# Routed experts of a top-1 mixture: eight windows of 256 to 320 slots ordered by their counts, with the up weights standing still

## The chip, the cores and the metric

The kernel runs on one core of one Trainium2 chip. The metric is the device time of one execution in microseconds. The median of several runs is compared.

## The reference

Two blocks stand one behind the other, each added to a residual stream `x` of 16 x 128 tokens with 256 values each. The first is a cross attention of 16 heads. The second, which the change is about, is a mixture of eight experts with one expert per token, beside one expert that all tokens share (cut to what matters; `x_aD` holds the 2048 tokens after a layer norm):

```python
scores_aE = x_aD @ router_DE                       # 2048 x 8
vals_aK, idx_aK = jax.lax.top_k(scores_aE, 1)
masked_aE = jnp.full_like(scores_aE, -jnp.inf).at[jnp.arange(a)[:, None], idx_aK].set(vals_aK)
gates_Ea = jax.nn.sigmoid(masked_aE).T
routed_in_EaD = gates_Ea[:, :, None] * x_aD[None, :, :]
mid_EaF = silu(einsum('ead,edf->eaf', routed_in_EaD, w1_eDF)) * einsum('ead,edf->eaf', routed_in_EaD, w3_eDF)
routed_out_EaD = einsum('eaf,efd->ead', mid_EaF, w2_eFD)
shared_aD = silu(x_aD @ ws1_DF) * (x_aD @ ws3_DF) @ ws2_FD
out_aD = shared_aD + routed_out_EaD.sum(axis=0)
```

The inner width F is 704 = 5 x 128 + 64. All data are float32.

## The kernel before, in words

**Order.** The order of every engine's instructions is the order of the program text (`manual_schedule`). There is no planner. The attention part comes first, pair by pair of batch rows. The shared expert (`hidden`, L164, and `down`, L181) is cut into units that a generator hands out (`shared_expert`, L196; `shared_unit`, L249). Some units are put between the last steps of the attention, and the others between the steps of the routing.

**Weights.** `load_experts` (L913), right behind the attention, has SP load w1, w3 and w2 of all eight experts, one expert after the other, and they stay (`w13s`, `wds`).

**Routing.** `route` (L943) is a generator too. The loop at L1243 takes one step of it, or two where the first says "chain", and then one unit of the shared expert. Its steps are small DVE operations: the best score and its expert for each token (`hit`), the counts on TensorE (L1001), prefix sums over the 16 tiles of tokens (`run`), the number of 128-slot tiles of each expert (`tiles`, L1011), their prefix sum (`upto`) and first slot (`base`), each token's slot (`slot`), and from it the tile and the row in it (`tile_f`, `row`). `past` and `expert` (L1041 to L1050) name the expert of each tile. `there` and `sent` (L1054, L1063) and one-hot rows (`find`, L1073: `at_row`) go through TensorE (L1082) and become the table of token numbers and gates by slot.

**Routed tiles.** Each expert's tokens fill tiles of 128 slots; NTILE = 23 is the most that can be needed, and this input needs 20. The work of one tile is spread over the steps of `tiles` (L1272):

- `gather` (L1119, POOL) fetches the rows of the tokens from `h_rows`, `gate` (L1131, DVE) multiplies by the gates.
- The first two tiles are turned on TensorE (`transpose_inputs`, L1134). The others are turned by DVE in 32 x 32 blocks (`turn_inputs`, L1142), stored to a DRAM tensor `x_blocks` and read back in the other block order (`fetch_inputs`, L1153), both by SP.
- `up` (L1160): the turned tokens stand still (`lhsT=xT`), the weights move in halves of 352 columns: two halves x w1 and w3 x two chunks of 128 inputs. SiLU on ACT (L1179) and the product on DVE (L1180) leave the hidden rows by token.
- `turn_hidden` (L1183) and `fetch_hidden` (L1202) turn them in the same way: DVE, DRAM (`m_blocks`), and back.
- `out_rows` (L1208): POOL gathers the stream's rows from `s_rows`, TensorE multiplies the turned hidden rows with w2 (L1221, six blocks), DVE adds (L1228), and POOL scatters the rows to `out` (L1230). It runs two tiles behind `up`.

Sixteen tiles are sure. Behind them, a branch on the number of used tiles (L1311) runs either up to tile 20 or up to tile 23. Each branch ends with `ending` (L1290): the shared expert's last 256 tokens (`held`, L219) lie between the last two tiles' down products, and they are added to the rows that the scatters left in `out`: SP reads the rows back behind all scatters (L228), DVE adds (L246), SP stores (L247).

**PSUM.** Two double banks (`ps_s`: the halves of `up`), three banks (`ps_m`: the shared expert and the turns), one (`ps_o`: the down product).

Of the kernel before, what the change touches and what calls it, by code (L numbers as in the profile page):

```python
# [9 lines left out]
F32 = mybir.dt.float32  # L10
# [7 lines left out]
P = 128  # L18
# [3 lines left out]
G = 128  # L22
# [3 lines left out]
def resampler_attn__then__top1_moe_kernel(  # L26
# [31 lines left out]

    NSUB = NT // G + E - 1
    NTILE = -(-NSUB * G // P)  # L60
    GP = P // G
    TB = 2 * P
    FH = F // 2
# [3 lines left out]
    assert G == P and NF % 2 == 0 and FR == 2 * BL and F <= 512 * 2  # L67
# [842 lines left out]
    w13s = wexp.tile([P, E, DC, 2 * F], F32, name="w13s")  # L910
    wds = wexp.tile([P, E, NF, D], F32, name="wds")

    def load_experts():  # L913
        for e in range(E):
            for n, w in enumerate((w1, w3)):
                nc.sync.dma_start(
                    out=w13s[:, e, :, n * F : (n + 1) * F],
                    in_=w[e].rearrange("(c p) f -> p c f", p=P),
                )
            nc.sync.dma_start(  # L920
                out=wds[:, e, 0:FC, :],
                in_=w2[e, 0 : FC * P, :].rearrange("(c p) d -> p c d", p=P),
            )
            nc.sync.dma_start(
                out=wds[:, e, FC, :],
                in_=w2[e, F - P : F, :].rearrange("(j k) d -> k j d", k=BL),
            )

    routing = {}

    def prefix(a, n, width, name):

        k = 1
        while k < n:
            o = mscratch.tile([P, n * width], F32, tag=name, name=f"{name}{k}", bufs=2)
            nc.vector.tensor_copy(o[:, 0 : k * width], a[:, 0 : k * width])
            nc.vector.tensor_tensor(
                o[:, k * width :], a[:, k * width :], a[:, 0 : (n - k) * width], ALU.add
            )
            a, k = o, 2 * k  # L940
        return a

    def route():  # L943

# [6 lines left out]
        num_i = mscratch.tile([P, NTILE * GP], I32, tag="ints", name="num_i")  # L951
        nc.gpsimd.iota(num_i, pattern=[[1, NTILE * GP]], base=0, channel_multiplier=0)
        num = mscratch.tile([P, NTILE * GP], F32, name="num")
# [16 lines left out]
        col = mscratch.tile([P, P], F32, name="col")  # L970
# [4 lines left out]
        pay = mscratch.tile([P, B, 2], F32, name="pay")  # L975
# [5 lines left out]
        hit = mscratch.tile([P, B, E], F32, name="hit")  # L981
# [25 lines left out]
        run = prefix(cnt[:, 1, :], B, E, "run")  # L1007
        yield "chain"
        total = run[:, (B - 1) * E :]
        tiles_i = mscratch.tile([P, E], I32, name="tiles_i")  # L1010
        nc.vector.tensor_scalar(tiles_i, total, float(G - 1), None, ALU.add)  # L1011
        nc.vector.tensor_scalar(tiles_i, tiles_i, G.bit_length() - 1, None, ALU.arith_shift_right)
        tiles = mscratch.tile([P, E], F32, name="tiles")
        nc.vector.tensor_copy(tiles, tiles_i)
        yield "chain"
        upto = prefix(tiles, E, 1, "upto")
        base = mscratch.tile([P, E], F32, name="base")
        nc.vector.tensor_tensor(base, upto, tiles, ALU.subtract)
        nc.vector.tensor_scalar(base, base, float(G), None, ALU.mult)
        yield "chain"  # L1020

        pos = mscratch.tile([P, B, E], F32, name="pos")
# [3 lines left out]
        nc.vector.tensor_tensor(pos, pos, base.unsqueeze(1).to_broadcast([P, B, E]), ALU.add)  # L1026
        nc.vector.tensor_tensor(pos, pos, hit, ALU.mult)
        yield "chain"
        slot = mscratch.tile([P, B], F32, name="slot")
        nc.vector.tensor_reduce(slot, pos, AX.X, ALU.add)  # L1030
        tile_i = mscratch.tile([P, B], I32, name="tile_i")
        nc.vector.tensor_copy(tile_i, slot)
        nc.vector.tensor_scalar(tile_i, tile_i, 7, None, ALU.arith_shift_right)
        tile_f = mscratch.tile([P, B], F32, name="tile_f")
        nc.vector.tensor_copy(tile_f, tile_i)
        row = mscratch.tile([P, B], F32, name="row")
        nc.vector.scalar_tensor_tensor(row, tile_f, -float(P), slot, ALU.mult, ALU.add)
        yield "chain"

        past = mscratch.tile([P, NTILE * GP, E], F32, tag="grid", name="past")  # L1040
        nc.vector.tensor_tensor(  # L1041
            past,
            upto.unsqueeze(1).to_broadcast([P, NTILE * GP, E]),
            num.unsqueeze(2).to_broadcast([P, NTILE * GP, E]),
            ALU.is_le,
        )
        expert = mscratch.tile([P, NTILE * GP], F32, name="expert")
        nc.vector.tensor_reduce(expert, past, AX.X, ALU.add)
        expert_i = mconst.tile([P, NTILE * GP], I32, name="expert_i")
        nc.vector.tensor_scalar(expert_i, expert, float(E - 1), None, ALU.min)  # L1050
        yield "chain"

        there = mscratch.tile([P, B, NTILE], F32, tag="grid", name="there")
        nc.vector.tensor_tensor(  # L1054
            there,
            num[:, 0:NTILE].unsqueeze(1).to_broadcast([P, B, NTILE]),
            tile_f.unsqueeze(2).to_broadcast([P, B, NTILE]),
            ALU.is_equal,
        )
        yield  # L1060
        sent = mscratch.tile([P, B, 2, NTILE], F32, name="sent")
        for k in range(2):
            nc.vector.tensor_tensor(  # L1063
                sent[:, :, k, :],
                there,
                pay[:, :, k : k + 1].to_broadcast([P, B, NTILE]),
                ALU.mult,
            )
            yield
        pt = ps_o.tile([P, 2, NTILE], F32, tag="O", name="slots")  # L1070
        at_row = {}

        def find(b):  # L1073
            at_row[b] = rwork.tile([P, P], F32, tag="xg" if b % 2 else "xp", name=f"at_row_{b}")
            nc.vector.tensor_scalar(at_row[b], col, row[:, b : b + 1], None, ALU.is_equal)

        find(0)
        find(1)
        yield
        for b in range(0, B, 2):  # L1080
            for k in (b, b + 1):
                nc.tensor.matmul(  # L1082
                    pt.rearrange("p k j -> p (k j)"),
                    lhsT=at_row.pop(k),
                    rhs=sent[:, k].rearrange("p k j -> p (k j)"),
                    start=(k == 0),
                    stop=(k == B - 1),
                )
            if b + 2 < B:
                find(b + 2)  # L1090
                find(b + 3)
                yield
        table = mconst.tile([P, NTILE], I32, name="table")
        nc.vector.tensor_scalar(table, pt[:, 0, :], float(NT), None, ALU.add)
        gates = mconst.tile([P, NTILE], F32, name="gates")
        nc.vector.tensor_copy(gates, pt[:, 1, :])
        used_i = mconst.tile([P, 1], I32, name="used_i")
        nc.vector.tensor_copy(used_i, upto[:, E - 1 : E])
        routing.update(expert=expert_i, table=table, gates=gates, used=used_i)
        for j in range(AHEAD):  # L1100
            gather(j)
        for _ in range(4):
            yield
        for j in range(AHEAD):
            gate(j)
        yield
        for j in range(2):
            transpose_inputs(j)
        gather(AHEAD)
        turn_inputs(2)  # L1110


    AHEAD = 3

    SURE, SHORT = NT // P, 20
    xTs, ups = {}, {}
    x_blocks = [tc.dram_tile([DC, NB, BL, NB, BL], F32, name=f"x_blocks_{k}") for k in range(3)]

    def gather(j):  # L1119
        xg = rwork.tile([P, D], F32, tag="xg", name=f"xg_{j}")  # L1120
        nc.gpsimd.indirect_dma_start(
            out=xg,
            out_offset=None,
            in_=h_rows,
            in_offset=Offset(ap=routing["table"][:, j : j + 1], axis=0),
            bounds_check=NT,
            oob_is_err=False,
        )
        xTs[j] = xg

    def gate(j):  # L1131
        nc.vector.tensor_scalar(xTs[j], xTs[j], routing["gates"][:, j : j + 1], None, ALU.mult)

    def transpose_inputs(j):  # L1134
        xg = xTs[j]
        px = ps_m.tile([P, DC, P], F32, tag="mm", name=f"px_{j}")
        for c in range(DC):
            nc.tensor.transpose(px[:, c, :], xg[:, ts(c, P)], ident)
        xTs[j] = rwork.tile([P, DC, P], F32, tag="xp", name=f"xT_{j}")
        nc.vector.tensor_copy(xTs[j], px)  # L1140

    def turn_inputs(j):  # L1142

        px = rwork.tile([P, DC, NB, BL], F32, tag="xp", name=f"xp_{j}")
        nc.vector.transpose(
            px, xTs[j].rearrange("p (c k j) -> p c j k", c=DC, k=BL)
        )
        nc.sync.dma_start(
# [209 lines left out]
```

## Time and profile before

| what | value |
|---|---|
| median of 3 runs | 755.81 us (755.73 to 755.83) |
| the profiled execution | 755.33 us, of which its span 753.6 us |
| granted clock of TensorE | 0.999 |
| first routed up product | 582.9 us from the start of the span |
| TensorE's last group | from 744.04, 5.34 us long |
| DMA | 142.48 MB, mean 189 GB/s |

A row of a timeline has the start in us, the length in us, the engine, the line, the operation, what it writes and reads, and how many instructions were merged; in brackets the idle time of its engine ahead of it and what ended it. TensorE's work shows as PE (the product) and PEld (the load of the standing operand). Every float32 product leaves two records. In a row of groups the busy time and the mean of one record follow the first bar, the idle time ahead of the group and its releaser the second. A DMA row ends with the size of one transfer and the median time from issue to landing.

### The profile page before, as it was taken

How to read it: one execution, taken by the hardware profiler on the slowest of the kernel's cores; microseconds unless marked ns; L12 is line 12 of the kernel's file. 1: busy time of each engine (PE TensorE's matmuls, PEld its weight loads, DVE VectorE, ACT ScalarE, POOL GpSimd, SP SyncE). 2: the span in 40 equal slices, each digit the busy share in tenths (PEclk: the TensorE clock that was granted, in tenths of full speed). 3: DMA queues.
4: the chain of work that ended last, by engine and by line, in shares of the span. 5: the costliest groups of instructions: out<-in, count | busy, mean ns of one | idle time of the engine just before them, and what ended most of it. 6: DMA issues, size and time to landing. Idle time of an engine off the chain costs nothing.

```text
span 753.6 us, 11767 instructions
## 1 busy us (share of the span) xinstructions
PE 744.9 (99%) x4062; PEld 572.3 (76%) x4062; DVE 414.9 (55%) x1012; ACT 258.9 (34%) x779; POOL 315.2 (42%) x366
## 2 busy tenths in 40 slices
PE   8999999999999999999999999999999999999997
PEld 6857768778677677677677687788888777777776
DVE  5566558458558647656646456535633454554431
ACT  2444433534444354364354355611211111111111
POOL 1363653563464355345445544611022334343331
PEclk9999999999999999999999999999999999999999
DMA  8075636835844943953853544543996577777751
GB/s 294 32 251 184 195 127 211 238 139 174 258 143 157 263 168 131 259 199 125 235 196 128 182 155 174 175 140 118 383 381 242 147 209 190 185 184 192 189 154 55
DMA packets 182066, 142.48 MB, mean 189 GB/s; under 512 B 95152, under 2 KB 165811, under 8 KB 182004
## 3 DMA queue, kind: packets, MB, share of 16 engines
q1 hardware_dynamic: 175460, 125.07, 53.2%
q0 software_dynamic: 4528, 13.18, 5.6%
q10 hardware_dynamic: 2016, 3.43, 1.3%
q8 instruction: 35, 0.57, 0.3%
q14 instruction: 27, 0.22, 0.1%
HBM read 84.50 MB, written 57.67 MB: 189 GB/s over the span
## 4 chain that ended last, share of the span: by engine, by line
PE 78%; DMA 12%; issue 4%; DVE 3%; ACT 2%; POOL 1%; POOLq 0%; SPq 0%; DVEq 0%; ACTq 0%
PE pk L440 15%; PE pv L459 14%; PE S L492 8%; PE O L557 8%; PE p L156 8%; PE pw L573 7%; PE pq L425 7%; DMA out_dram<-sg,table 6%; DMA sg<-s_rows,table 5%; PE ys L186 5%; PE u L1169 3%; PE yr L1221 1%; ACT pe L511 1%; PE pr L628 1%; PE pr L156 1%
## 5 line engine op out<-in xcount | busy, mean ns | idle before, releaser
L524 POOL TENSOR_SCALAR pe<-pe,rs 128x256 f32<-128x256 f32 x256 | 233.0, 929 | 246.0 <-DVE rs L521 246.0
L511 ACT ACTIVATE pe<-S,nmx 128x256 f32<-128x256 f32 x256 | 118.9, 490 | 132.5 <-DVE nmx L504 132.5
L459 PE MATMUL pv<-wv,kvT 128*128 128x512 f32 x256 | 116.5, 599 | 0.2 <-ACT kT L448 0.2
L440 PE MATMUL pk<-kvT,wk 128*128 128x256 f32 x512 | 115.0, 382 | 1.3 <-ACT kT L448 0.7
L440 PEld LDWEIGHTS pk<-kvT,wk 128*128 128x128 f32 x512 | 95.9, 190 | 19.1 <-DVE px L533 2.0
L533 DVE STREAM_TRANSPOSE px<-pe 128x512 f32<-128x512 f32 x128 | 81.4, 683 | 32.5 <-POOL pe L524 32.4
L1169 PE MATMUL u<-w13s,xT 128*128 x320 | 97.8, 459 | 0.0
L459 PEld LDWEIGHTS pv<-wv,kvT 128*128 128x128 f32 x256 | 47.2, 190 | 53.2 <-issue 50.6
L1169 PEld LDWEIGHTS u<-w13s,xT 128*128 128x128 f32 x320 | 60.8, 190 | 30.7
L504 DVE TENSOR_REDUCE nmx<-S 128x4 f32<-128x1024 f32 x64 | 75.1, 1214 | 8.7 <-PE S L492 8.5
L156 PE MATMUL p<-hT,ws 128*128 128x256 f32 x320 | 73.8, 382 | 0.7 <-DVE mid L172 0.7
L156 PEld LDWEIGHTS p<-hT,ws 128*128 128x128 f32 x320 | 59.9, 190 | 10.6 <-DVE mid L172 1.7
L557 PEld LDWEIGHTS O<-pT,v 128*64 128x64 f32 x1024 | 55.2, 137 | 14.7 <-issue 12.9
L492 PE MATMUL S<-kT,qT 64*128 64x256 f32 x512 | 63.9, 389 | 0.0
L1179 ACT ACTIVATE rsl<-u 128x352 f32<-128x352 f32 x40 | 18.6, 464 | 130.6 <-PE u L1169 130.6
L557 PE MATMUL O<-pT,v 128*64 128x128 f32 x1024 | 63.0, 276 | 0.0
L521 DVE RECIPROCAL rs<-sums 128x4 f32<-128x4 f32 x64 | 11.4, 178 | 93.7 <-ACT pe L511 93.7
L466 ACT COPY v<-pv 128x512 f32<-128x512 f32 x64 | 38.2, 599 | 62.9 <-PE pv L459 62.9
L573 PEld LDWEIGHTS pw<-wo,oT 128*128 128x128 f32 x256 | 48.6, 190 | 12.2 <-issue 3.1
L573 PE MATMUL pw<-wo,oT 128*128 128x256 f32 x256 | 57.9, 379 | 0.0
L425 PE MATMUL pq<-kvT,wq 128*128 128x256 f32 x256 | 57.7, 379 | 0.0
L511 ACT ACTIVATION_READ_ACCUMULATOR pe<-S,nmx 128x1 f32 x256 | 56.5, 221 | 0.0
(203 smaller groups left out, 784.4 us busy)
## 6 DMA issues: line engine op xcount, KB each, us to landing
p_blocks<-px SPq DMA_DIRECT2D x64, 512.0 KB, 2.9
pT<-p_blocks SPq DMA_DIRECT2D x64, 512.0 KB, 4.2
w13s<-in_w_dram SPq DMA_DIRECT2D x16, 704.0 KB, 10.8
m_blocks<-body SPq DMA_DIRECT2D x20, 384.0 KB, 2.5
mT<-m_blocks SPq DMA_DIRECT2D x20, 384.0 KB, 4.0
wds<-in_w_dram SPq DMA_DIRECT2D x8, 640.0 KB, 12.4
t_blocks<-tx SPq DMA_DIRECT2D x12, 256.0 KB, 2.8
kvT<-t_blocks SPq DMA_DIRECT2D x12, 256.0 KB, 5.9
```

What stands on the lines that cost most here:

```text
L156: nc.tensor.matmul(ps, lhsT=shared["w13"][:, c, ds(col, P)], rhs=hT[:, c, ts(t, TB)], start=(c == 0), stop=(c == DC - 1),)
L425: nc.tensor.matmul(pq[:, jj], lhsT=wq[:, c, ts(2 * j + jj, P)], rhs=kvTs[g][:, c, :, 1, :], start=(c == 0), stop=(c == DC - 1),)
L440: nc.tensor.matmul(pk[:, jj, :], lhsT=wk[:, c, ts(2 * j + jj, P)], rhs=kvTs[b // 2][:, c, b % 2].rearrange("p t s -> p (t s)"), start=(c = ...
L459: nc.tensor.matmul(pv, lhsT=kvTs[b // 2][:, c, b % 2, t, :], rhs=wv[:, c, ts(n, 512)], start=(c == 0), stop=(c == DC - 1),)
L492: nc.tensor.matmul(pl[:, r, j, :], lhsT=qTs[b // 2][rows, k, b % 2, :], rhs=kTs[b][rows, k, :], start=True, stop=True,)
L504: nc.vector.tensor_reduce(nmx, pl, AX.X, ALU.max, negate=True)
L511: nc.scalar.activation(pes[u][:, h, :], pl[:, r, j, :], AF.Exp, bias=nmx[:, r, j : j + 1], accum_out=sums[u][:, h : h + 1],)
L524: nc.gpsimd.tensor_scalar(w, w, rs[:, i : i + 1], None, ALU.mult)
L533: nc.vector.transpose(px[:, :, t].rearrange("p j h q -> p h j q"), pes[u][:, ts(n, 4), ts(t, S)].rearrange("p h (j k) -> p h j k", k=BL),)
L557: nc.tensor.matmul(o[r * HD : (r + 1) * HD, j, :], lhsT=vs[b][:, t, ts(2 * (4 * half + j) + r, HD)], rhs=pTs[u][:, j // 2, :, t, 2 * (j % ...
L573: nc.tensor.matmul(pw, lhsT=outT[2 * b + k // 4][:, k % 4, :], rhs=wo[:, k, :], start=(k == 0), stop=(k == NP - 1))
L1169: nc.tensor.matmul(pl[:, m, 0:FH], lhsT=xT[:, c, :], rhs=w13s[:, ds(e, 1), c, ds(m * F + n * FH, FH)].rearrange("p e f -> p (e f)"), start ...
```

## The change

Each expert gets one **window** of slots. The windows have fixed sizes, 320, 288, 288, 288, 256, 256, 256 and 256, and the experts are put to them in the order of their counts, the largest first. A window consists of two tiles of 128 slots and, in the first four, a rest of 64 or 32; the sixteen full tiles have numbers 0 to 15 and the rests 16 to 19. If an expert has more tokens than its window has slots, a branch at the end takes the tokens beyond (`overflow`, up to 14 more tiles of 128).

- **Up products.** The weights stand still, in blocks of 128 columns, and the turned tokens of a whole window move. The hidden rows come out turned, as the down product needs them, so `turn_hidden`, `fetch_hidden` and `m_blocks` go. Block 5 holds the last 64 columns of w1 and of w3 side by side, and for this w3's columns are stored in another order.
- **Weights.** w2 of all experts is loaded ahead as before. w1 and w3 are loaded by SP for one window at a time into three buffers, the first three during the routing as soon as the experts are ordered, the others two windows ahead. SP reads the expert's number from a register.
- **Order in a window.** Behind the first block come the turning of the next window's inputs, the gathers for the window after it, the down products of the window before, the fetch of the next inputs and the load of weights. The down products' PSUM comes from `ps_m`.
- **Routing.** `tiles`, `upto`, `base`, `past` are replaced by ranks of the counts (`key`, `more`, `window`), by a place in the expert and a window for each token (`place`, `win`), by the tokens beyond (`over`) and by the largest load (`most`), on which the branch depends.
- **Ending.** `held` follows the last window; its first block comes before that window's down products, all others behind them.

The diff, cut to its core:

```diff
-G = 128
+WINDOWS = (320, 288, 288, 288, 256, 256, 256, 256)
...
-    w13s = wexp.tile([P, E, DC, 2 * F], F32, name="w13s")
     wds = wexp.tile([P, E, NF, D], F32, name="wds")
+    w13s = [wexp.tile([P, DC, 2 * F], F32, name=f"w13_{k}") for k in range(3)]
...
+        total = run[:, (B - 1) * E :]
+        key = mscratch.tile([P, E], F32, name="key")
+        nc.vector.scalar_tensor_tensor(key, total, float(2 * E), rank, ALU.mult, ALU.add)
+        more = mscratch.tile([P, E, E], F32, tag="grid", name="more")
+        nc.vector.tensor_tensor(
+            more,
+            key.unsqueeze(1).to_broadcast([P, E, E]),
+            key.unsqueeze(2).to_broadcast([P, E, E]),
+            ALU.is_gt,
+        )
+        window = mscratch.tile([P, E], F32, name="window")
+        nc.vector.tensor_reduce(window, more, AX.X, ALU.add)
+        yield "chain"
...
+        nc.vector.tensor_tensor(pos, pos, hit, ALU.mult)
+        own = mscratch.tile([P, B, E], F32, tag="own", name="own")
+        nc.vector.tensor_tensor(own, hit, window.unsqueeze(1).to_broadcast([P, B, E]), ALU.mult)
+        place = mscratch.tile([P, B], F32, name="place")
+        nc.vector.tensor_reduce(place, pos, AX.X, ALU.add)
+        win = mscratch.tile([P, B], F32, name="win")
+        nc.vector.tensor_reduce(win, own, AX.X, ALU.add)
+        yield "chain"
+        slot = mscratch.tile([P, B], F32, name="slot")
+        nc.vector.scalar_tensor_tensor(slot, win, 2.0 * P, place, ALU.mult, ALU.add)
...
+        over = beyond(place, win, B, "over", mconst)
...
+        for n, _ in enumerate(finding):
+            if n == 0:
...
+                nc.vector.tensor_copy(expert_i, expert)
+                for w in range(3):
+                    load_up(w, w)
+            if n == 1:
+                load = beyond(total, window, E, "load", mconst)
+                most = mscratch.tile([P, 1], F32, name="most")
+                nc.vector.tensor_reduce(most, load, AX.X, ALU.max)
...
+            yield
...
+        for i, t in enumerate(tiles_of(0)):
+            transpose_inputs(t, inputs_t[0][:, :, ds(i * P, rows_of(t))], rows_of(t))
+        for t in tiles_of(1):
+            gather(t)
...
+    def turn_inputs(w):
+        for i, t in enumerate(tiles_of(w)):
+            n = rows_of(t)
+            gate(t)
+            px = rwork.tile([P, DC, NB, BL], F32, tag="xp", name=f"xp_{t}")
+            nc.vector.transpose(
+                px[0:n], xgs.pop(t)[0:n, :].rearrange("p (c k j) -> p c j k", c=DC, k=BL)
+            )
+            nc.sync.dma_start(
+                out=x_blocks[:, ds(i * NB, n // BL)].rearrange("c i k j q -> (i k) c (j q)"),
+                in_=px[0:n].rearrange("p c j q -> p c (j q)"),
+            )
+
+    def fetch_inputs(w):
+        n = WINDOWS[w]
+        for c in range(DC):
+            nc.sync.dma_start(
+                out=inputs_t[w % 2][:, c, 0:n].rearrange("p (i q) -> p i q", q=BL),
+                in_=x_blocks[c, 0 : n // BL].rearrange("i k j q -> (k j) i q"),
+            )
+
+    def load_up(k, w):
+        e = nc.sync.value_load(routing["expert"][0:1, w : w + 1], min_val=0, max_val=E - 1)
+        a1, a3 = (a[ds(e, 1)].rearrange("e (c p) f -> p (e c) f", p=P) for a in (w1, w3))
+        nc.sync.dma_start(out=w13s[k][:, :, 0:F], in_=a1)
+        nc.sync.dma_start(out=w13s[k][:, :, F : F + FR], in_=a3[:, :, FC * P : F])
+        nc.sync.dma_start(out=w13s[k][:, :, F + FR : 2 * F], in_=a3[:, :, 0 : FC * P])
+
+    def up(w13, xT, n, mid, f, name):
+        ps = ps_s.tile([P, 2, 512], F32, tag="S", name=f"u_{name}_{f}")
+        sl = mwork.tile([P, WMAX], F32, tag="sl", name=f"rsl_{name}_{f}")[:, 0:n]
+        for k, col in enumerate((f * P, F + FR + f * P) if f < FC else (FC * P,)):
+            for c in range(DC):
+                nc.tensor.matmul(
+                    ps[:, k, 0:n],
+                    lhsT=w13[:, c, ds(col, P)],
+                    rhs=xT[:, c, 0:n],
+                    start=(c == 0),
+                    stop=(c == DC - 1),
+                )
+        if f < FC:
+            nc.scalar.activation(sl, ps[:, 0, 0:n], AF.Silu)
+            nc.vector.tensor_tensor(mid[:, f, 0:n], ps[:, 1, 0:n], sl, ALU.mult)
+        else:
+            hi = slice(P - FR, P)
+            nc.scalar.activation(sl[hi, :], ps[0:FR, 0, 0:n], AF.Silu)
+            nc.vector.tensor_tensor(mid[hi, FC, 0:n], ps[hi, 0, 0:n], sl[hi, :], ALU.mult)
...
+    for w in range(E):
+        ups[w] = nc.tensor.value_load(
+            routing["expert"][0:1, w : w + 1], min_val=0, max_val=E - 1
+        )
+        for f in range(NF):
+            up(w13s[w % 3], inputs_t[w % 2], WINDOWS[w], mids[w % 2], f, f"w{w}")
+            if f == 0:
+                sgs = [stream_rows(t, rows_of(t)) for t in tiles_of(w - 1)] if w else []
+                if w + 1 < E:
+                    turn_inputs(w + 1)
+                if w + 2 < E:
+                    for t in tiles_of(w + 2):
+                        gather(t)
+                if w:
+                    down_window(w - 1, sgs)
+                else:
+                    shared_unit()
+                if w + 1 < E:
+                    fetch_inputs(w + 1)
+                if 1 <= w < E - 2:
+                    load_up((w + 2) % 3, w + 2)
+
+    def ending():
+        rest = held(mids[E % 2][:, :, 0:TB])
+        sgs = [stream_rows(t, rows_of(t)) for t in tiles_of(E - 1)]
+        next(rest)
+        down_window(E - 1, sgs)
+        for _ in rest:
+            pass
...
+    with tc.If(most <= 2 * P) as cmp:
+        ending()
+    with cmp.Else():
+        scattered[:] = done
+        overflow()
+        ending()
```

`stream_rows` is the gather from `s_rows` that `out_rows` did before; `down_window` calls `out_rows` for the two or three tiles of a window; `tiles_of` and `rows_of` give a window's tiles and their rows.

## The prediction, before the changed kernel was run

> **What bounds the kernel now.** I read the page first: its busy line, then its costliest groups. TensorE is busy for nearly the whole span, and the routed part is 320 records of the up product (L1169) and 240 of the down product (L1221).
>
> ```profile
> PE 744.9 (99%) x4062; PEld 572.3 (76%) x4062; DVE 414.9 (55%) x1012; ACT 258.9 (34%) x779; POOL 315.2 (42%) x366
> ...
> L1169 PE MATMUL u<-w13s,xT 128*128 x320 | 97.8, 459 | 0.0
> ...
> L1169 PEld LDWEIGHTS u<-w13s,xT 128*128 128x128 f32 x320 | 60.8, 190 | 30.7
> ...
> L156 PE MATMUL p<-hT,ws 128*128 128x256 f32 x320 | 73.8, 382 | 0.7 <-DVE mid L172 0.7
> ```
>
> The last number of each row is the idle time before that group. The up product waits for nothing. A mean of 459 ns per record is no price, since records overlap. The price is the pace, which the timeline of TensorE alone gives from one start to the next:
>
> ```profile
> 692.75 4.90 PE L1169 MATMUL u<-w13s,xT 128*128 x16
> 697.48 2.75 PE L1221 MATMUL yr<-wds,mT 128*128 x12
> 700.07 4.90 PE L1169 MATMUL u<-w13s,xT 128*128 x16
> ...
> 733.68 7.07 PE L156 MATMUL p<-hT,ws 128*128 128x256 f32 x32
> 740.59 2.75 PE L1221 MATMUL yr<-wds,mT 128*128 x12
> ```
>
> Sixteen up records take 697.48 - 692.75 = 4.73 us, 0.2956 each with 352 moving columns. Twelve down records take 2.59, 0.2158 each with 256. The shared expert's 32 take 6.91, also 0.2159 each with 256. So a record costs 0.2158 us plus 0.831 ns for each column over 256 (0.0798/96). The stage has no gap until the end: its length is the sum of TensorE's records, and anything that DVE, the queues or the DMAs save there is worth nothing.
>
> **The up product.** Each product shows as two records. Before: 20 tiles x 16 records x 0.2956 = 94.6 us. After: the weights stand, and a window's slots move. A window has 11 column blocks of 128 (1408 in all), 2 chunks, 2 records: 44. At 320, 288 and 256 columns the formula gives 0.2690, 0.2424 and 0.2158 us. The sum is 44 x (0.2690 + 3 x 0.2424 + 4 x 0.2158) = 44 x 1.8594 = 81.8 us. **Gain 12.8 us.** In columns: 352 x 2208 against 320 x 352, 14% fewer. The reason is the last block: 64 columns of w1 and 64 of w3 share one stationary block, and slots are padded less.
>
> Here a rule speaks against the change. Perfetto Trace Analysis, "Identifying the Most-Contended Engine", says that matmul occupancy is a bad measure of headroom and that the share of time spent loading weights is the good one. The change adds 32 loads and shortens the move that covers each: by that rule, at 190 ns a load, 6.1 us are added. The row decides: L156 has the planned form (128 weights standing, 256 moving) and keeps 0.2159 with its 190 ns loads. The move, not the load, sets the pace; I take the 12.8.
>
> **The down product.** Before 20 tiles, after 16 full tiles and 4 short ones (64, 32, 32, 32 rows). The 256 weight columns still move through each, so a short tile costs a whole 12 x 0.2158. 20 x 2.59 both times: 0. The four short tiles save nothing.
>
> **Work taken off.** The turn of the hidden rows (DVE, 80 transposes at L1189 and L1193, 34.7 us in the groups of this stage), its 20 stores and 20 fetches and 12 of TensorE's 20 register loads go. All lay beside TensorE: 0.
>
> **New waits in the up product.** The blocks rotate through two PSUM pairs, and the last block of a window is short (4 records), so the next window's first block asks for a pair that was filled only 4 records before. The shared expert shows how long an evacuation takes:
>
> ```profile
> 737.34 0.38 ACT L171 ACTIVATE sl<-p 128x256 f32<-128x256 f32 x1 [1.34 <-PE p L156]
> 737.75 0.42 DVE L172 TENSOR_TENSOR body<-p,sl 128x256 f32<-128x256 f32 x1 [1.00 <-ACT sl L171]
> ```
>
> That block's 8 records end at 733.68 + 16 x 0.2158 = 737.13; SiLU starts 0.21 later and DVE's product ends at 738.17, 1.04 after the end. Restarting TensorE took about 0.16 (DVE ended at 574.97, the next group started at 575.03 and ran 0.10 longer). Inside a window 1.20 fits into a block's 1.73. At the boundary only 4 x 0.2158 = 0.86 covers it: 0.33 us idle. With 288 and 320 slots SiLU and product grow (up to 0.46 and 0.52 at 352), the short block too: 0.28 and 0.24. Seven boundaries: 0.24 + 3 x 0.28 + 3 x 0.33 = **+2.1 us**. Bounds: 0 if the framework frees a pair earlier, 3.5 if restarting costs twice as much.
>
> TensorE's register load stands at the same boundary, behind the short block. It is dispatched once the block before has started its last 0.7 us, so 0.7 + 0.86 + 0.33 = 1.9 us cover it. No row shows one alone. The nearest is the old branch near 705 us, whose load and jump held POOL 1.6 us and DVE 0.9: 0, at worst +0.5 at a boundary if the cover is gone. The new branch ahead of the ending has 1.55: 0, at worst 0.5.
>
> **The route.** The loop has as many steps as before (23 of 25 units), but DVE's steps are heavier. Before, DVE was nearly the limit:
>
> ```profile
> 533.49 8.80 PE L156 MATMUL p<-hT,ws 128*128 128x256 f32 x40
> ...
> 534.30 0.16 DVE L1011 TENSOR_SCALAR tiles_i<-run 128x8 int32<-128x8 f32 x1
> ...
> 542.12 1.03 PE L156 MATMUL pr<-hT,ws 128*128 128x256 f32 x4
> ...
> 542.74 0.42 DVE L172 TENSOR_TENSOR mid<-p,sl 128x256 f32<-128x256 f32 x1 [0.64 <-ACT sl L171]
> 543.08 0.47 DVE L1075 TENSOR_SCALAR at_row<-col,row 128x128 f32<-128x128 f32 x2
> ...
> 543.41 0.64 PE L1082 MATMUL slots<-sent,at_row 128*128 128x46 f32 x4 [0.26 <-DVE at_row L1075]
> ```
>
> From 534.30 to the row search DVE is idle for 0.64 us only. By the pitch of starts, an operation on up to 16 values costs 0.20, on 64 values 0.24, on 128 values 0.32, on 320 to 368 some 0.5. The old tiles, prefix and base lasted 1.86; the new key, ranks, places and windows (3 small, 6 of 128) 2.58. Slot steps: 2.33 against 2.84 (14 small). Grid and expert: 1.30 against 1.40. Payload: 0.45 against 1.68, since six small steps for the experts' loads lie there. That is +2.5; less the idle 0.64, the row search starts 1.9 us later and TensorE's slots product, which waits for it in order, with it. **+1.9 us**; bounds 0.5 and 2.5.
>
> **First window.** Three transposes instead of two take all three ps_m buffers. TensorE already waited 0.49 us there for DVE's L172; now the third transpose takes that buffer and the next block waits for DVE's first copy, 0.36 later, plus 0.1 of transposes: **+0.5**, bounds 0 and 1.
>
> **Weights in order.** SP first loads w2 (6.3 MB, from 522.5 to some 539 at 381 GB/s), then waits for the experts' names (about 541.7 us), then loads three pairs of w1 and w3 (1.44 MB each). At the same 381 GB/s these land near 541.7 + 11.4 = 553, needed near 584: 0. Behind SP's wait stand only window 1's stores, 30 us later. A later pair has nearly two windows (over 28 us); at this stage's 190 GB/s it needs 8. 0.
>
> **Window inputs.** They still go through DRAM, now just in time. The page's DMA rows:
>
> ```profile
> x_blocks<-xp SPq DMA_DIRECT2D x18, 128.0 KB, 3.7
> xT<-x_blocks SPq DMA_DIRECT2D x18, 128.0 KB, 4.2
> ```
>
> For windows 6 and 7, counted from the end of the first block: product 1.04, two gates and turns 2.0, store 3.7, two fetches 4.2 and some 2 for the second = 12.9 us. Cover: two down tiles 5.2, the other blocks 36 x 0.2158 = 7.8, the gap 0.3 = 13.3. It just fits; longer windows leave more. 0, but with the slowest landings (5.0 and 5.0) windows 6 and 7 would be 2.2 late each, window 1 2 and windows 2 to 4 0.7: up to +8.5.
>
> **The end.** Before, the last scatter started at 744.09, and reading it back made DVE's last add wait:
>
> ```profile
> 749.09 0.42 DVE L246 TENSOR_TENSOR xr<-ys,xr 128x256 f32<-128x256 f32 x1 [4.01 <-DMA xr<-out_dram]
> 749.54 1.47 SPq L247 DMA_DIRECT2D out_dram<-xr  x2
> 749.75 0.42 DVE L246 TENSOR_TENSOR xr<-ys,xr 128x256 f32<-128x256 f32 x1 [0.24 <-DMA xr<-out_dram]
> ```
>
> TensorE's last group ends at 744.04 + 5.34 = 749.38. After, five blocks (7.8 us) stand behind the last down tile, so the rows are back before and the add starts at once: -0.33, and the second store no longer queues behind the first. **-0.5**, bounds -0.8 and 0.
>
> **Sum.** -12.8 + 2.1 + 1.9 + 0.5 - 0.5 = -8.8 us. The profiled execution took 755.33 (span 753.6 and 1.7 around it), so 746.5; it lay 0.5 below the median of the runs, 755.81, so **747.0 us**.
>
> **Rivals.** (1) No bubbles: a pair comes free early and the route's extra DVE work hides, leaving -12.8 to -12.3, 743.3 us. For it: seldom more than one engine is late here. Against it: DVE's single 0.64. 17%. (2) Some covers fail: a few window inputs or register loads are late, +3.5 us, 750.5. For it: 0.4 us of room at windows 6 and 7. 20%. (3) Slower: the trip of the window inputs through DRAM becomes the bound. A window's fetch is issued after its stores have landed, so each window can start late by itself. Beyond 8.8/7 = 1.3 us on each of seven starts the gain is gone; 2.2 on each gives 15.4 - 8.8, 762.4. Against it: only the slowest landings on record, all at once, reach break-even, and the queue now carries no hidden rows. 5%; a further 3% ends near no change. (4) That the overflow path runs: the reference's router on its inputs gives 312, 286, 264, 262, 239, 232, 228 and 225 tokens, which fit the windows in order. Fourteen tiles at 44 x 0.109 + 2.6 = 7.4 us would add over 100; I leave it out.
>
> **How the numbers follow.** The sum as worked out has 55%. The range from 742.8 to 751.0 holds it with rival 1 and most of rival 2, and leaves out the rest. About 0.2% (1.5 us) is what a measurement can tell from no change. Faster 0.92, same 0.03, slower 0.05.
>
> **What would show it.** Right: 352 up records at 0.216 to 0.269 us, 240 down records at 0.216, gaps of about 0.3 us ahead of each window's first block released by DVE's product, a gap of 2 us ahead of the slots product, no wait of DVE's last add for the DMA. Wrong: up records at another pace, a window's start released by the DMA of its inputs, or w13 waited for.

## The result, and the profile after

The changed kernel takes 748.42 us (748.27 to 748.73, 4 runs) against 755.82 beside it: a ratio of 0.9902, 95% interval 0.9885 to 0.9919. The forecast was 747.0, range 742.8 to 751.0. The profiled execution took 748.45 with a span of 746.6; the span fell by 7.0 us.

The page after, its busy line and the two rows of the up product:

```profile
PE 736.0 (99%) x4096; PEld 572.5 (77%) x4096; DVE 385.8 (52%) x949; ACT 259.1 (35%) x787; POOL 314.4 (42%) x366
...
L1249 PE MATMUL u_w<-xT,w 128*128 128x256 f32 (+2 forms) x352 | 85.6, 399 | 0.3
L1249 PEld LDWEIGHTS u_w<-xT,w 128*128 128x128 f32 x352 | 66.0, 190 | 18.8 <-DVE mid_w L1258 3.3
```

TensorE is as full as before. The 352 up records are there, and now their weight loads wait for DVE. The view of waits (what waited, for whom, us in total, times, longest) has

```profile
PEld u_w L1249 <- DVE mid_w L1258: 3.3, 7, 0.5
```

A load runs ahead of the products, so TensorE itself loses less than the 3.3 us: 2.12, as experiment 3 shows. DVE's busy time fell by 29 us, and none of that shows in the span.

The timeline of TensorE gives the lengths by starts. The first and the last row are the first up product and the last shared down product. Between them stand a window of 288 slots with its neighbours' down products, then windows of 256 up to the ending:

```profile
584.11 2.32 PE L1249 MATMUL u_w<-xT,w 128*128 128x320 f32 x8
...
622.39 8.05 PE L1279 MATMUL yr<-wds,mid_w 128*128 x36
630.37 11.23 PE L1249 MATMUL u_w<-xT,w 128*128 128x288 f32 x44
641.43 8.05 PE L1279 MATMUL yr<-wds,mid_w 128*128 x36
...
698.37 10.00 PE L1249 MATMUL u_w<-xT,w 128*128 128x256 f32 x44
708.21 5.34 PE L1279 MATMUL yr<-wds,mid_w 128*128 x24
713.39 7.93 PE L1249 MATMUL u_w<-xT,w 128*128 128x256 f32 x36
721.16 1.89 PE L162 MATMUL p<-hT,ws 128*128 128x256 f32 x8
...
735.83 5.34 PE L245 MATMUL ys<-wsd,mid_w 128*128 128x256 f32 x24
```

A row of 44 holds five blocks of one window and the first of the next, so the boundary lies in it. The last row of 36 holds none: 721.16 - 713.39 = 7.77 = 36 x 0.2158, the pace of the formula exactly. The rows with a boundary are longer than their records: 9.84 instead of 9.50, and 11.06 instead of 10.67. The 36 down records of a three-tile window take 630.37 - 622.39 = 7.98, where 36 x 0.2158 is 7.77.

The other places that the prediction named: the slots product in the timeline of TensorE, the window inputs in the view of DMA issues of the routed part (transfer size and median time to landing at the end), and the end in the timeline of all engines.

```profile
542.42 1.03 PE L162 MATMUL pr<-hT,ws 128*128 128x256 f32 x4
544.29 0.64 PE L983 MATMUL slots<-sent,at_row 128*128 128x40 f32 x4 [0.84 <-DVE at_row L976]
```

```profile
x_blocks<-xp SPq DMA_DIRECT2D x14, 128.0 KB, 2.0
...
xT<-x_blocks SPq DMA_DIRECT2D x8, 128.0 KB, 3.0
```

```profile
739.08 2.93 SPq L253 DMA_DIRECT2D out_dram<-xr  x2
741.22 0.42 DVE L252 TENSOR_TENSOR xr<-ys,xr 128x256 f32<-128x256 f32 x1 [2.17 <-PE ys L245]
```

TensorE waits for DVE's row search, 0.84 us instead of 0.26. The inputs land sooner than before, and no row of TensorE waits for them. The last add waits for TensorE and no longer for the DMA.

The span's change, put together from starts of TensorE's rows:

| stretch | before | after | change | forecast |
|---|---|---|---|---|
| start to the first up product | 582.90 | 584.11 | +1.2 | +2.4 |
| first up product to the last shared down product | 161.14 | 151.72 | -9.4 | -10.7 |
| from there to the end of the span | 9.56 | 10.77 | +1.2 | -0.5 |

Of the first +1.2, 0.3 was there by 16 us, in the loading of the first inputs; in the runs below it was 0.1 to 0.9, so it belongs to no edit. Ahead of the slots product 0.6 were lost, at the third transpose 0.3. The second stretch repeats well: it is 151.72 or 151.73 us in the changed kernel, in its repetition and in experiments 1 and 5, which leave it as it is. So a difference of a few hundredths can be read there, while the intervals of the ratios below hardly part edits that lie 1.5 us from each other.

### The profile page after: what moved, and what is told of

It reads as the page before. It is cut to its first block, busy times and chain, and to the rows that moved or that the text cites. A ratio compares the mean times of both kernels' runs of the same rounds, so it can differ in the third digit from the quotient of the medians.

```text
span 746.6 us, 11560 instructions
## 1 busy us (share of the span) xinstructions
PE 736.0 (99%) x4096; PEld 572.5 (77%) x4096; DVE 385.8 (52%) x949; ACT 259.1 (35%) x787; POOL 314.4 (42%) x366
## 4 chain that ended last, share of the span: by engine, by line
PE 93%; DVE 4%; ACT 2%; issue 0%; DMA 0%; ACTq 0%
PE pk L446 15%; PE pv L465 14%; PE u_w L1249 11%; PE S L498 8%; PE O L563 8%; PE p L162 8%; PE pw L579 7%; PE pq L431 7%; PE yr L1279 7%; PE ys L192 5%; ACT pe L517 1%; PE pr L634 1%; PE pr L162 1%; PE ys L245 1%; PE slots L983 0%
## 5 line engine op out<-in xcount | busy, mean ns | idle before, releaser
L1249 PE MATMUL u_w<-xT,w 128*128 128x256 f32 (+2 forms) x352 | 85.6, 399 | 0.3
L1249 PEld LDWEIGHTS u_w<-xT,w 128*128 128x128 f32 x352 | 66.0, 190 | 18.8 <-DVE mid_w L1258 3.3
L1257 ACT ACTIVATE rsl_w<-u_w 128x256 f32<-128x256 f32 (+2 forms) x40 | 16.0, 400 | 118.8 <-PE u_w L1249 118.8
```

The source lines that it names most:

```text
L1249: nc.tensor.matmul(ps[:, k, 0:n], lhsT=w13[:, c, ds(col, P)], rhs=xT[:, c, 0:n], start=(c == 0), stop=(c == DC - 1),)
```

## The experiments

Each is an edit of the changed kernel. The ratio is to the kernel before, with its 95% interval.

**1. Where does the end go?** DVE's last add no longer waits for the DMA, as forecast. Still the program ends later. The raw records of SP show what stands between (start in us, length, operation, line of the branch or of the program's end):

```
before   751.07   0.04 COMPARE_BRANCH   L1311
         751.57   0.02 EVENT_SEMAPHORE  L1354
after    742.41   0.04 COMPARE_BRANCH   L1432
         745.02   0.02 EVENT_SEMAPHORE  L1474
```

Behind its last store SP leaves the branch by a jump over the other side, and its next instruction comes 0.5 us later before, 2.6 us later after. The DMA view of the changed kernel from 741 us on has the queues that load instructions:

```profile
q1 hardware_dynamic: 144, 0.13, 7.9%
q14 instruction: 3, 0.02, 1.4%
q8 instruction: 1, 0.02, 1.0%
```

The first experiment leaves the branch away:

```diff
-    (_, (most,)) = nc.values_load_multi_w_load_instructions(
-        routing["most"][0:1, 0:1], min_val=1, max_val=NT
-    )
     done = list(scattered)
-    with tc.If(most <= 2 * P) as cmp:
-        ending()
-    with cmp.Else():
-        scattered[:] = done
-        overflow()
-        ending()
+    ending()
```

> The branch and the overflow path are left out (no token of this input lies beyond its window), so the ending follows the last window directly. Theory 'jump': in the changed kernel SP leaves the branch by a jump over the overflow code, 2.6 us pass before its next instruction, and the program's closing waits start that much later. Without it the stretch from DVE's last add to the end of the span falls from 5.0 us to about 3.0, the time from 748.4 to about 746.4. Rival 'store': the last store's landing sets the end. Then nothing changes: 748.4, the stretch stays at 5.0.

Measured: 746.73 us, 0.9878 (0.9861 to 0.9894). The same DMA view has one queue left:

```profile
q1 hardware_dynamic: 144, 0.13, 10.4%
```

From TensorE's last group to the end there are now 744.8 - 735.85 = 8.95 us instead of 10.77. "Jump" holds, "store" falls: the loss is 1.8 us. It is less than 2.6 because a part of the jump lay beside the last store: without the branch SP waits at this place from 742.14 to 743.41, and the last packets of the store end at 743.05. So the end alone would have changed by 8.95 - 9.56 = -0.6, where -0.5 was forecast.

**2. The sides of the branch exchanged.**

```diff
-    with tc.If(most <= 2 * P) as cmp:
-        ending()
-    with cmp.Else():
-        scattered[:] = done
-        overflow()
-        ending()
+    with tc.If(most > 2 * P) as cmp:
+        overflow()
+        ending()
+    with cmp.Else():
+        scattered[:] = done
+        ending()
```

> The two sides of the branch change places: the overflow side stands first, the usual side last, so that the usual path jumps on entry and runs out of the program's end without a jump. Theory 'jump': the end gains what the kernel without overflow gains, some 2 us; on entry TensorE has 1.55 us of queued work to cover a jump of up to 2.6, so up to 1.0 is lost there: 746.4 to 747.4. Rival 'store': 748.4, or slower by a gap of TensorE ahead of the ending.

Measured: 750.98 us (748.99 to 751.71), 0.9936 (0.9920 to 0.9953): a miss. The end is 747.2 - 738.25 = 8.95 us long, as expected, but the timeline of TensorE shows the entry:

```profile
713.18 7.93 PE L1249 MATMUL u_w<-xT,w 128*128 128x256 f32 x36
723.47 1.99 PE L162 MATMUL p<-hT,ws 128*128 128x256 f32 x8 [2.35 <-issue]
```

TensorE's own jump lasts 3.5 us by its record (719.88 to 723.42), not 2.6, and only the five records queued behind its start, 1.1 us, covered it. This wait with the label "issue" is such time: no semaphore is late. The kernel before had shown the size: by the raw records TensorE's jump at its end lasts 3.75 us (from 745.36), hidden by 17 queued records. The profiled execution is the fastest of the four, 748.99; why the others took some 2 us more no trace here shows.

**3. The pair of banks at the window's boundary.**

```diff
-        ps = ps_s.tile([P, 2, 512], F32, tag="S", name=f"u_{name}_{f}")
+        if f < FC:
+            ps = ps_s.tile([P, 2, 512], F32, tag="S", name=f"u_{name}_{f}")
+        else:
+            ps = ps_m.tile([P, 1, 512], F32, tag="mm", name=f"u_{name}_{f}")
```

> The short block 5 of each window takes one of the three ps_m banks and no longer one of the two pairs, so the next window's first block finds a pair whose product ended a whole block earlier. Theory 'pair': the seven gaps of 0.25 to 0.44 us ahead of each window's first block, 2.6 us in all, are waits for DVE's product on block 4: they go, 745.9 us. Rival 'register': they are TensorE's load of the expert's number at the same place: they stay, 748.4.

Measured: 746.33 us, 0.9871 (0.9854 to 0.9887). The seven waits for DVE are gone from the view of waits, and the timeline of TensorE has

```profile
697.05 9.66 PE L1252 MATMUL u_w<-xT,w 128*128 128x256 f32 x44
706.54 5.34 PE L1282 MATMUL yr<-wds,mid_w 128*128 x24
```

9.49 for 44 records, the pure pace. From the first up product to the last shared down product there are 734.17 - 584.57 = 149.60 us instead of 151.72: the seven gaps were 2.12 us. "Pair" holds; the register load, in the same place, costs nothing. With 288 slots 0.1 us a window stays, which the next experiment explains.

**4. The narrow standing blocks of the rests.**

```diff
-    mids = [hidden_t.tile([P, NF, WMAX], F32, name=f"mid_w{k}") for k in range(2)]
+    mids = [hidden_t.tile([P, NF, 3 * P], F32, name=f"mid_w{k}") for k in range(2)]
...
+        nc.gpsimd.memset(mid[:, :, 2 * P : 3 * P], 0.0)
...
-                py[0:n, :],
-                lhsT=mid[:, f, 0:n],
+                py,
+                lhsT=mid[:, f, 0:P],
...
-            out_rows(t, rows_of(t), ups[w], mids[w % 2][:, :, ds(i * P, rows_of(t))], sg)
+            out_rows(t, rows_of(t), ups[w], mids[w % 2][:, :, ts(i, P)], sg)
```

> The down products of the four rests of 64 and 32 slots run with a standing block of full width (128 columns, the ones beyond the rest cleared once and their results not read). Theory 'shape': a narrow standing block costs 0.21 to 0.23 us beside the 2.59 of a whole tile[...]; with full width the 36 records of a three-tile window take 7.77 us instead of 7.98 to 8.00, and the time falls by 0.85 to 747.6. Rival 'third tile': three tiles in a row cost it for another reason (a PSUM bank, an add): 748.4, 7.98 us stays.

Measured: 747.51 us, 0.9887 (0.9871 to 0.9904). The timeline of TensorE around the same window:

```profile
641.18 7.93 PE L1279 MATMUL yr<-wds,mid_w 128*128 x36
648.95 10.91 PE L1249 MATMUL u_w<-xT,w 128*128 128x288 f32 x44
```

The down products take 648.95 - 641.18 = 7.77. The up row behind them, too, is 0.11 shorter than in the changed kernel. The stretch of the table is 734.95 - 584.51 = 150.44 us, 1.28 shorter: 0.32 for each of the four rests, 0.21 in its own records and 0.11 in those behind. The view of waits of the changed kernel names four waits at each of the two places, and none of them is left here:

```profile
PEld u_w L1249 <- issue: 1.6, 4, 0.4
PEld yr L1279 <- issue: 1.3, 4, 0.3
```

"Shape" holds in place and is half as large again as expected. The time is only 0.9 lower: the profiled execution has a start 0.4 us longer than the changed kernel's, which the edit doesn't touch, and of the other runs there is no trace. That the width of the standing block costs this is shown by the edit; why it does is not, as the trace's label is "issue".

**5. Two pieces of the routing later.**

```diff
-            if n == 0:
+            if n == 4:
                 named = mscratch.tile([P, E, E], F32, tag="named", name="named")
...
-            if n == 1:
+            if n == 6:
                 load = beyond(total, window, E, "load", mconst)
```

> The naming of the experts (with the first three loads) comes four steps of the routing later and the largest load five, behind the first row searches. Theory 'DVE': TensorE's wait of 0.84 us ahead of the first slots product comes from these two pieces, some 2.1 us of DVE time in a stretch where DVE has no idle time; moved, the wait falls to the 0.26 of the kernel before or less, the time by some 0.6 to 747.8. Rival 'PE': the row search waits for the product on TensorE's own last block in any order; the wait stays at 0.8, 748.4. The first weights then land some 9 us later, near 562, still 20 us early.

Measured: 748.07 us, 0.9896 (0.9879 to 0.9912). In the timeline of TensorE the wait ahead of the slots product is back at the value of before:

```profile
543.06 1.03 PE L162 MATMUL pr<-hT,ws 128*128 128x256 f32 x4
544.35 0.64 PE L983 MATMUL slots<-sent,at_row 128*128 128x40 f32 x4 [0.26 <-DVE at_row L976]
```

"DVE" holds, with 0.6 us in the trace (the changed kernel's wait was 0.84). In the time itself 0.4 are too near the spread of the runs to prove it (the start of the profiled execution happened to be 0.6 us longer). The next experiment bears it out from another side: its windows are of one size, so four small DVE steps fall away, and the wait there is 0.27 us.

**6. All windows of 320 slots.**

```diff
-WINDOWS = (320, 288, 288, 288, 256, 256, 256, 256)
+WINDOWS = (320,) * 8
```

> All eight windows have 320 slots: same weights standing, same 352 records, more columns. Theory 'columns': a record costs 0.2158 us plus 0.831 ns a column over 256, so 352 records at 0.2690 are 94.7 us against 81.8, +12.9; four more rests at 12 x 0.2158 and 0.32 for the narrow block, +11.6; boundary gaps 0.4 shorter: 772.5. Rival 'records': the number of products and loads sets the up product; it stays, and only the rests add: 760.

Measured: 772.1 us, 1.0219 (1.0202 to 1.0236). "Columns" holds within 0.4 us. The 2560 slots are as many as the 20 tiles of before have, and by the formula the up product is then as long as before, 94.7 us against 94.6. So in the up product standing weights gain nothing by themselves; the gain is the slots that the smaller windows leave out (2208). The 16 us above the kernel before are, by an estimate from the figures above, for the larger part the four more tiles of the down product (10.4 us) and eight narrow blocks (2.6).

**7. Do the loads set the pace?**

```diff
     def up(w13, xT, n, mid, f, name):
         ps = ps_s.tile([P, 2, 512], F32, tag="S", name=f"u_{name}_{f}")
+        n = P
...
-        nc.gpsimd.memset(mid[0 : P - FR, FC, :], 0.0)
+        nc.gpsimd.memset(mid, 0.0)
```

> The up products move only the first 128 slots of each window; the hidden rows of all other slots are left at zero, so their part of the computation is left out. Every weight load stays, with 128 columns to cover it. Rule 'load' (loads of 190 ns set the pace): records 0.190 us apart inside a block, about 731 us. Theory 'move': 0.2158 - 128 x 0.00083 = 0.109 us apart inside a block; the blocks of 0.88 then wait for the 1.2 us of evacuation, about 1.04 each, and the time falls to some 715.

Measured: 726.5 us, one run. The timeline of TensorE at the last window:

```profile
694.97 4.31 PE L1250 MATMUL u_w<-xT,w 128*128 128x128 f32 x36
699.13 1.99 PE L162 MATMUL p<-hT,ws 128*128 128x256 f32 x8
```

36 records start within 4.16 us, 0.116 each; the first block of all (584.66 to 585.55) had 0.111. That is near the formula's 0.109, and far from 0.190. The loads are all there, and by the page's row one is longer than this pace, so they overlap each other:

```profile
L1250 PEld LDWEIGHTS u_w<-xT,w 128*128 128x128 f32 x352 | 45.5, 205 | 17.9 <-DVE mid_w L1259 7.9
```

So "load" falls, by the pace; the time alone would not tell, as 726.5 lies nearer to 731 than to 715. It is 11 us above what "move" expected, and the view of waits has


```profile
PE u_w L1250 <- DVE mid_w L1259: 6.2, 9, 2.2
PE u_w L1250 <- DVE sg L1287: 2.9, 1, 2.9
PE u_w L1250 <- DMA xT<-x_blocks: 2.3, 2, 1.4
PE u_w L1250 <- issue: 1.7, 1, 1.7
```

With less work to cover them, waits that the prediction costed at nothing come forward: 13.1 us, of which 9.1 are for DVE (its product on a block, and once behind its add for the down product), 2.3 for the windows' inputs and 1.7 have no releaser. "Move" itself had put in some 0.16 us of waiting for each block, so how much of the 11 us each of them makes is not settled.

**8. The branch ahead of the last window's later blocks.** The usual side stands last, as in 2.

```diff
                 if 1 <= w < E - 2:
                     load_up((w + 2) % 3, w + 2)
+            if w == E - 1:
+                break
+
+    def last_window():
+        w = E - 1
+        for f in range(1, NF):
+            up(w13s[w % 3], inputs_t[w % 2], WINDOWS[w], mids[w % 2], f, f"w{w}")
...
-    with tc.If(most <= 2 * P) as cmp:
-        ending()
-    with cmp.Else():
-        scattered[:] = done
-        overflow()
-        ending()
+    with tc.If(most > 2 * P) as cmp:
+        last_window()
+        overflow()
+        ending()
+    with cmp.Else():
+        scattered[:] = done
+        last_window()
+        ending()
```

> The branch stands behind the first block of the last window and the down products of the window before it, with the overflow side first and the usual side last. Theory 'jump': on entry 24 queued records of 5.2 us cover TensorE's jump of 3.5, and the program ends without one: the stretch from the last add to the end is 3.1 us instead of 5.0, TensorE has no gap of 2.4, 746.6 us. Rival 'other engines': a jump of DVE, SP or POOL of the same size delays the product on the next block and TensorE waits for it up to 2 us: 748.5.

Measured: 748.0 us, 0.9897 (0.9881 to 0.9914): neither theory in full. The end is 746.3 - 737.37 = 8.93 us, but in the timeline of TensorE two gaps have come:

```profile
714.16 3.69 PE L1249 MATMUL u_w<-xT,w 128*128 128x256 f32 x16 [0.45 <-PE yr L1279]
718.27 4.58 PE L1249 MATMUL u_w<-xT,w 128*128 128x256 f32 x20 [0.41 <-DVE mid_w L1258]
```

By the records TensorE's sequencer reaches the branch at 710.09, when 8 of the 24 queued records have run, and jumps until 713.92; the rest of the queue covers only 3.5 us of that. DVE jumps from 714.87 to 717.72 and is late with the next product. The gain is 1.8, the loss 1.4: the stretch of the table is 153.10 us instead of 151.72.

**9 to 11. Together.** Edits 3, 4 and 5; the same with 8; the changed kernel once more.

> Three edits together on the changed kernel: the short block in a ps_m bank, the rests' standing blocks at full width, the naming and load steps of the routing later. If the three losses (2.1 us of boundary gaps, 1.3 of narrow blocks, 0.6 ahead of the slots product) are separate, as each theory has it, they add: 4.0 less than the changed kernel, 744.4. Rival 'one cover': removing one lets another wait (window inputs, at windows 6 and 7) come forward; then 745.5 or more and a wait for the inputs' DMA.

> The three edits and the branch ahead of the last window's later blocks. Alone, the early branch gained 1.9 at the end and lost 1.4 to the jumps on entry (TensorE 3.8 us, DVE 2.9). If these add: 0.4 below the kernel with the three edits, 744.0. Rival: with the pair's wait gone the entry costs the same or more, no gain, 744.4 or above.

> The changed kernel itself, once more, beside the two: 748.4, and 0.990 of the kernel before.

Measured: 744.54 us, 0.9852 (0.9837 to 0.9867); 743.88 us, 0.9842 (0.9828 to 0.9855); 748.49 us, 0.9902 (0.9887 to 0.9917). The three losses add (3.95 us below the changed kernel beside it, 4.0 expected), and no new wait takes their place. The stretch of the table, with the three edits,

```profile
583.35 2.32 PE L1252 MATMUL u_w<-xT,w 128*128 128x320 f32 x8
...
731.67 5.34 PE L245 MATMUL ys<-wsd,mid_w 128*128 128x256 f32 x24
```

is 148.32 us, 3.40 shorter than in the changed kernel, where 2.12 and 1.28 were found alone. The early branch adds some 0.7. The intervals overlap, but all five of its runs (743.80 to 744.04) lie below the four without it (744.16 to 745.11). Its trace agrees: the stretch is 1.36 us longer, at 149.68, and the end 1.91 shorter, 8.92 instead of 10.83. The version with all four is the fastest of all and beats both kernels.

## Why the prediction was right, point by point

- **Up product, -12.8: right.** The sum is borne out by the stretch itself: -12.78 + 2.12 (experiment 3) + 1.28 (experiment 4) = -9.4, as measured; with both losses gone it is 148.32 - 161.14 = -12.82. Experiment 6 changes the columns and the number of rests and lands within 0.4 us; experiment 7 rules out that loads of 190 ns set the pace. Two points of its working do not hold. The columns are 44 x 2208, not 352 x 2208, against 320 x 352 (the 14% is right). And these 14% are the slots alone: with 2560 slots the two products are equal, so the shared last block only keeps the new form from being longer. As to the rule set against the change: the Trainium skill, Perfetto Trace Analysis, "Identifying the Most-Contended Engine", names the share of weight loads together with MFU, the matmul arithmetic done as a share of the peak, and puts no price on a load; the 6.1 us were the prediction's own reading. The share went from 76 to 77% here.
- **New waits at the boundary, +2.1: right**, 2.12, at the seven places named, released by DVE's product on block 4.
- **The down product, 0: wrong by 1.3.** The sum counted only the moving columns of the short tiles. A standing block of another width than its neighbours costs 0.32 us more, which no row of the routed part before could show, as all its tiles were whole.
- **The route, +1.9: place right, size wrong**, 0.6. The failing term is the pitch of DVE's steps. Taken were 0.32 us for 128 values and 0.20 for up to 16, as they follow when each waits for the one before. The new steps are partly independent of each other, and then the next starts before the last has ended: from 534.60 to 536.63 the nine steps of ranks and places took 2.03 us, not 2.58; the later pieces 2.55, 1.24 and 1.47 instead of 2.84, 1.40 and 1.68.
- **First window, +0.5: nearly right**, 0.3, with the waits at the third transpose and behind it as named.
- **The end, -0.5: the cause held, and it was not all.** The add starts at once and the stretch would have been 0.6 shorter; but the step named only the branch's entry and left out its exit. SP's jump over the overflow side costs 1.8. The Trainium skill, Runtime: NRT & Kernel Launch, "Instruction fetch mechanics", states that a taken branch to a page that isn't loaded stalls until a DMA has fetched it. The instruction packets in the end of the changed kernel's trace and their absence without the branch agree with it. But the kernel before has five such packets from 744 us on, and its SP jumped in 0.5 us, so why the jump became 2.1 us longer stays open.
- **Inputs, weights, register loads, 0: right.** No row of TensorE waits for them. The POOL reading beside it was not: its 1.6 us near 705 ended, by the view, with DVE's product (L1180); by the raw records load and jump took 0.66 us (704.24 to 704.90) of that engine, beside a scatter still under way. The store of inputs landed in 2.0 us and the fetch in 3.0 where 3.7 and 4.2 were taken, so the room at windows 6 and 7 was larger than 0.4.
- **Rivals.** None of the slow cases came, and of the covers of rival 2 none failed in the changed kernel; experiment 7, which shortens the products that cover them, shows that they were no idle worry.
- **The net.** The span fell by 7.0 us where 8.8 were forecast. Taken too dear were the route (-1.3) and the first window (-0.2); missed were the narrow blocks (+1.3), the exit of the branch (+1.7 against the forecast end) and 0.3 at the start of this execution: +1.8. The medians lie 7.4 apart. Errors of -1.5 and +3.3 partly cancelled, which is luck, so the close total proves less than the stretches do.

## What to carry to other kernels

When one engine is full, price a change by the pace of that engine's records in the row that has the new form, and then look for what the new order takes from under it: here, every short step in a rotation of buffers, every odd tile width and every jump. Work it out for the end of the program as well: a branch is paid on leaving as on entering, and by whichever engine has no queued work left. An overflow path that never runs still costs its jump.

## What the runs showed of the hardware that was not expected

- A standing block of 32 or 64 columns between blocks of 128 cost TensorE 0.32 us, 0.21 in its own twelve records and 0.11 behind them.
- At the program's end SP's next instruction came 0.50 us behind its jump in the kernel before and 2.61 in the changed one, ACT's 0.44 and 2.47, DVE's 0.56 and 0.55; TensorE's own record of the jump lasts 3.75 and 3.41. On entering the last side TensorE's lasts 3.5 (experiment 2) and 3.8 (experiment 8), and DVE's next instruction came 2.85 behind its own (experiment 8). So the larger side does not lengthen every engine's jump.
- TensorE's sequencer reached these jumps with 16 or 17 records still to start, 3.5 to 3.9 us ahead of the end of its queued work (the ends of both kernels, experiments 8 and 10); in experiment 2 it was 5 records.
- With 128 moving columns float32 records followed each other in 0.111 us, though a weight load lasts 205 ns by its row (experiment 7).
